# A convolution block on one Trainium2 core: small weights loaded in the first chunks, group matrices loaded by halves and copied, set-up products padded to 64 rows

## The chip, the core and the metric

The kernel runs on one core of a Trainium2 chip. A core has five engines, each with an instruction queue of its own: TensorE (PE in the profile: matrix products from on-chip memory into accumulators; its weight loads are listed as PEld), VectorE (DVE), ScalarE (ACT), GpSimd (POOL) and SyncE (SP), which here only issues DMAs. An engine waits for another, or for a DMA, by semaphores. The DMAs issued by SyncE, ScalarE and GpSimd are carried out by 16 DMA engines. On-chip memory has 128 partitions; an image's channels or pixels lie along them.

The metric is the time of one execution on the device in microseconds (us), and of several runs the median.

## What is computed

Sixteen images of 192 channels and 64x64 pixels in float32 go through two layers. The reference, cut to what matters:

```python
h = layer_norm_over_channels(x)
projected, gate = split(conv1x1(h, in_proj_w, in_proj_b))        # 192 -> 2 x 192
projected = depthwise_3x3(projected, dw_k)
scanned = sum_d mix[d] * scan(projected * iscale[d], decay[d])   # left, right, down, up
local = depthwise_3x3(projected, le_k)
mixed = gelu(batch_norm((scanned + local) * sigmoid(gate)))
x = x + conv1x1(mixed, out_proj_w, out_proj_b)
x = x + fc2(gelu(fc1(layer_norm_over_channels(x))))              # 192 -> 768 -> 192
# second layer
t = relu(norm(mean_over_pixels(x) @ w1.T))
taps = (t @ w2.T + b2) * mask                                    # four taps per channel and image
out = depthwise_3x3(x, taps) + bias
```

The change touches how the weights of `conv1x1(in_proj)` and of the depthwise convolutions are prepared and loaded, not what is computed from them.

## The kernel before

The program has three stages, written one after the other.

**First stage** (lines 278 to 643): normalisation and input projection. The work is cut into 64 chunks, n = 0 to 63; four chunks make a block, and 16 blocks cover all images. The loop at line 617 emits, for each chunk n, in this order on every queue:

- `load_a(n + 3)` (line 502): six DMAs of 128 KB bring the pixels of the chunk three ahead into one of four buffers xa, three issued by SyncE and three by GpSimd. It waits until chunk n - 1 is done with the buffer.
- the stores of the block before. In a block's first chunk these are `store_first` (line 565) and parts 0 and 1 of `store` (line 580), in its second, third and fourth chunk one further part each. Half of the DMAs are issued by SyncE, half by GpSimd. So the last store of a block is issued in the fourth chunk of the next one.
- `turn(n + 1)` (line 515): 24 TensorE transposes of the next chunk, for its variance.
- `project(n, ...)` (line 537): four groups of six matmuls with 64-row operands and 128-column weights into accumulators of which two alternate (`ps_pj0`, `ps_pj1`). VectorE (line 555) and ScalarE (line 556) scale each group and write it into the block's buffer: `stg` for even blocks, part of `mid` for odd ones. Each is one buffer: block 12 writes `stg` again, which block 10 filled and which is free when the stores of block 10 have read it. Block 12 begins at n = 48, block 13 at 52, block 14 at 56.
- the functions that `beside(n, f)` (line 458) put down for this chunk: they come last in it.

These functions prepare the rest of the program. `diagonals`, `gate_bias`, `decay_rows`, `projection_bias` (line 349), `tap_sums`, `columns` (370), `sums_across` (375) and `conv_bias` (381) build biases from small matmuls in chunks 2 to 23. `projection_bias` has nine matmuls of 64x64 weights with one moving column; `conv_bias` runs three times (n = 19, 21, 23) with operands of three rows, `indt` and `svt`, which lie in the room of a later weight, `wf1`. In the trace one float32 matmul is two records, with a weight load of its own each. `vector` and `store_vector` build vectors of convolution taps and decays and store them in device memory (`dv_d`, `lv_d`).

From these vectors `load_dm(g)` (line 216) and `load_lm(g)` (line 223) load the banded matrices of channel group g: every partition reads a run that begins one place earlier than its neighbour's. `dm` (64 rows by 64 columns for 3 x 8 channels) is needed on partitions 0 to 63 and again, the same data, on 64 to 127; half 0 is issued by SyncE, half 1 by GpSimd. For `lm` the two halves hold different channels. `load_weights(k)` (line 111) loads the small weights of later stages, all issued by SyncE: k = 0 output projection, k = 3 and 4 squeeze weights and parameters, k = 1 and 2 the large ones.

**Second stage** (lines 646 to 863): depthwise convolution, scans and gate for 24 groups of eight channels, in 96 steps k of two channels. `depthwise(k)` multiplies by `dm`, `scans(k)` runs on VectorE with `tables(k)` made by ScalarE, `local` and `vertical` multiply by `lm`, `gate` multiplies and stores. Step k = 0 also has `hidden_bias` and `squeeze_rows`. `depthwise(4)`, the first to read group 1's matrices, is emitted in step k = 2.

**Third stage** (from line 866): output projection, second normalisation, hidden layer and the second layer's convolution. The change does not touch it.

The order on every engine is that of the program text; nothing is reordered by a planner.

Of the kernel before, what the change touches and what calls it, by code (L numbers as in the profile page):

```python
# [22 lines left out]
AF = mybir.ActivationFunctionType  # L23
# [4 lines left out]
C = 192  # L28
# [28 lines left out]
def conv_block_kernel(ctx: ExitStack, tc: tile.TileContext, x, prm, w_in, w_out, w_fc1, b_fc1, w_fc2, w1, bn1, w2, out):  # L57
    nc = tc.nc
# [5 lines left out]
    HALF = (slice(0, 64), slice(64, 128))  # L64
# [23 lines left out]
    pt3 = cp.tile([128, 3, NPRM], F32, tag="pt3", name="pt3")  # L88
# [54 lines left out]
    def squeeze_rows(pr):  # L143

        nc.tensor.matmul(pr[:, 0:2 * RED], ones[0:RED], sq_d.rearrange("p k r -> p (k r)"), start=True, stop=True)
        nc.vector.tensor_mul(w1t, w1t, pr[:, 0:RED].unsqueeze(1).broadcast_to([128, 3, RED]))
        nc.vector.tensor_copy(c0, pr[:, RED:2 * RED])
# [57 lines left out]
    mats = [{"dm": ce.tile([128, 3, HW, GC], F32, tag=f"dm{i}", name=f"dm{i}")} for i in range(2)]  # L205
# [10 lines left out]
    def load_dm(g, halves=(0, 1)):  # L216
        for i in halves:
# [2 lines left out]
            src = bass.AP(v.tensor, v.offset, [[GC, HW], [128 * GC, 3], [1, HW * GC]])  # L220
            (nc.sync, nc.gpsimd)[i].dma_start(mats[g % 2]["dm"][q].rearrange("p k m c -> p k (m c)"), src)

    def load_lm(g, halves=(0, 1)):
        n = GC // 2
        for i in halves:
            q = HALF[i]
            v = lv_d[g, i, :, 0:1, :]
            src = bass.AP(v.tensor, v.offset, [[n, HW], [128 * n, 5], [1, HW * n]])
            (nc.sync, nc.gpsimd)[i].dma_start(lm_of(g)[q].rearrange("p k m c -> p k (m c)"), src)
# [48 lines left out]
    with ExitStack() as stage:  # L278
# [3 lines left out]
        lo = slice(0, 64)  # L282

        w0 = place[:, 0:NFC * C].rearrange("p (t n) -> p t n", t=3)
        room = wf1.rearrange("p t m -> p (t m)")
        cut = lambda p, at_, n: room[0:p, at_:at_ + n]
        dg = cut(64, 768, 576).rearrange("p (t k n) -> p t k n", t=3, k=3)
        lnb = cut(64, 1344, 384).rearrange("p (t n) -> p t n", t=3)
        mean_w = cut(64, 0, 128)
        indt, svt = cut(3, 1984, 128), cut(3, 2112, C)  # L290
        dec = ka.tile([64, 3, 4], F32, tag="dec", name="dec")
        bp = ka.tile([64, 3], F32, tag="bp", name="bp")
        sv = ka.tile([64, 3, 3, 3], F32, tag="sv", name="sv")
# [2 lines left out]
        def bank():  # L296
            return psa.tile([128, CH], F32, tag="pj0", name="pb", bufs=2)
# [51 lines left out]
        def projection_bias():  # L349
            pbp = bank()  # L350
            for t in range(3):
                for u in range(3):
                    nc.tensor.matmul(pbp[lo, t:t + 1], w0[lo, u, 64 * t:64 * t + 64], pt3[lo, u, LN1B:LN1B + 1],
                                     start=(u == 0), stop=(u == 2))
            nc.vector.tensor_add(bp, pbp[lo, 0:3], pt3[lo, :, INB])
            nc.vector.memset(ind, 1.0)
            nc.vector.tensor_add(ind[:, 1:2], ident[:, 63:64], ident[:, 127:128])
            nc.vector.tensor_add(ind[:, 2:3], ident[:, 0:1], ident[:, 64:65])

        def tap_sums(t):  # L360
# [6 lines left out]
            nc.gpsimd.tensor_scalar_mul(sv[:, t], sv[:, t], bp[:, t:t + 1])  # L367
            nc.gpsimd.tensor_scalar_mul(sv[:, t, :, 1:3], sv[:, t, :, 1:3], -1.0)

        def columns():  # L370
            pi = bank()
            nc.tensor.transpose(pi[0:3, 0:128], ind, ident)
            nc.scalar.activation(indt, pi[0:3, 0:128], AF.Copy)

        def sums_across(k):
            pr = bank()
            for t in range(3):
                nc.tensor.transpose(pr[0:3, 64 * t:64 * t + 64], sv[:, t, k], ident[lo, lo])
            nc.scalar.activation(svt, pr[0:3, 0:C], AF.Copy)

        def conv_bias(k):
            pq = bank()
# [75 lines left out]
        def beside(n, f, *args):  # L458
            side.setdefault(n, []).append((f, args))
# [6 lines left out]
        beside(7, projection_bias)  # L466
        for t in range(3):
            beside(8 + t, tap_sums, t)
        beside(8, columns)
        for k in range(3):  # L470
            beside(18 + 2 * k, sums_across, k)
            beside(19 + 2 * k, conv_bias, k)
        for k, n in enumerate((13, 14, 15, 16, 24, 32, 33, 34)):
# [3 lines left out]
                    beside(n + j, ready, j // 2, j % 2)  # L477
                    beside(n + 1 + j, runs, j // 2, j % 2)
            beside(n + (5 if k == 4 else 1), store_vector, k)
        for k in (0, 3, 4):  # L480
            beside(40 + k, load_weights, k)
        for h in range(2):
            beside(46 + 4 * h, load_dm, 0, (h,))
            beside(54 + 4 * h, load_lm, 0, (h,))
        beside(60, load_dm, 1)
        beside(61, load_lm, 1)
        beside(62, load_weights, 1)
        beside(50, squeeze_scale)
# [128 lines left out]
        for n in range(n_ac):  # L617
# [11 lines left out]
            h = AR // 2 if n == 0 else 0  # L629
# [16 lines left out]
    with ExitStack() as stage:  # L646
# [11 lines left out]
        def load_pg(g, queue=nc.sync, i0=0, i1=n_half):  # L658
            s = grp[g]
            s["pg"] = pg_even if g % 3 == 0 else pg_odd[g % 3 - 1]  # L660
            if g:
                d = [lo_ <= g < hi_ for lo_, hi_ in PARTS].index(True)
                lo_ = (g - PARTS[d][0]) * GE
                queue.dma_start(s["pg"].rearrange("p n k c j -> p n (k c j)")[:, i0 * NB:i1 * NB],
                                pg_d[d][i0:i1, :, :, lo_:lo_ + GE].rearrange("i b p e -> p (i b) e"))
# [29 lines left out]
        def tables(k):  # L695

            bst[k]["tab"] = []
            for d in range(2):
                tab = wb.tile([128, 2 * CH], F32, tag=f"tab{d}", name=f"tab{d}")
                nc.scalar.activation(tab.rearrange("p (n h) -> p n h", h=HW), mask[:, d].broadcast_to([128, n_img_all, HW]),  # L700
                                     AF.Copy, scale=dec_b[:, d, k:k + 1])
                bst[k]["tab"].append(tab)
# [28 lines left out]
        def vertical(k):  # L731
            for d in range(2):
                lmul(k, 3 + d, lambda h, ih: bst[k]["v"][d][h, ih], lambda a: a, False, d == 1)
# [81 lines left out]
        for k in range(-2, n_bp + 1):  # L815
            if k == -2:
                tables(0)
            elif 0 < k + 1 < n_bp:
                tables(k + 1)
            if k >= 1:  # L820
                vertical(k - 1)
                gate(k - 1)
                g, c = divmod(k, hp_)
                if c == 0 and 0 < g < NCG - 1:
                    load_lm(g + 1)
                if c == 0 and g == 3:
                    load_weights(2)
                if c == 0 and g + 2 < NCG:
                    load_pg(g + 2)
                if c == hp_ - 2 and g + 2 < NCG:  # L830
                    load_dm(g + 2)
            if 0 <= k + 1 < n_bp:
                scans(k + 1)
            if k + 2 < n_bp:
                depthwise(k + 2)
            if 0 <= k < n_bp:
                local(k)
                sigmoid(k)
            if k == 0:
                pb_h = psb.tile([128, 2, CH], F32, tag="d", name="pb_h", bufs=2)  # L840
                hidden_bias(pb_h)
                squeeze_rows(pb_h[:, 0, HCH:CH])
            if k in (1, 3, 5):
                scale_hidden(k // 2)
            if k == n_bp - hp_:

                nc.gpsimd.dma_start(w2t, w2[:, 0:NTAP, :])
                load_y(0, y_low, (nc.sync,), (0, 1))
                load_x2(0)
                load_x2(1)  # L850
            if k == n_bp - hp_ // 2:
                load_y(0, y_low, (nc.sync,), (2,), LASTC)
# [467 lines left out]
    for n in range(n_ch + 1):  # L1320
        p, c = divmod(n, NCH)
# [159 lines left out]
```

## Time and profile before

| | |
|---|---|
| median of three runs | 3539.12 us (3538.75 to 3540.4) |
| the profiled execution | 3536.52 us |
| its span, first to last instruction | 3534.7 us |
| mean granted TensorE clock | 0.997 of full speed |
| first stage | to about 582 us |
| second stage | about 582 to 1250 us |
| third stage | from there to the end |

The page gives busy times and shares of the span for each engine, then the chain of work that ended last: from the last instruction back, at each step, to what released it. A group of instructions is written with its line, engine and operation, and the tiles as out<-in; x48 is the count. A bracket after a line of the timeline is the idle time of that engine before it and the engine or DMA to which the wait is put down; that name is inferred. Matmul lines overlap, since matmuls are pipelined: distances are taken from start to start. Lines SPq are DMA issues of SyncE; the time there is that of the issue, not of the transfer.

### The profile page before, as it was taken

The page shows a single profiled execution, that of the slowest core. Times are in us where ns is not written, and L with a number is a line of the kernel's source. Part 1 is how long each engine was busy: PE and PEld are TensorE (multiplying, and loading weights), DVE is VectorE, ACT ScalarE, POOL GpSimd, SP SyncE. Part 2 cuts the span into 40 slices and gives each one's busy share as a digit, 9 for nine tenths or more (in the row PEclk, how much of TensorE's full clock was granted, in tenths as well). Part 3 has the DMA queues.
Part 4 walks back from the last instruction along what each step waited for, and adds up shares of the span by engine and source line. Part 5 has one row for each costly group of instructions (what it writes and reads, how often), then busy time and mean ns, then how long its engine had stood idle before and what let it go on. Part 6 is the DMA issues. An engine that isn't in the chain of part 4 may idle for free.

```text
span 3534.7 us, 78563 instructions
## 1 busy us (share of the span) xinstructions
PE 3505.9 (99%) x33158; PEld 1910.7 (54%) x33158; DVE 2740.9 (78%) x4669; ACT 1840.2 (52%) x2087; POOL 1171.4 (33%) x1302
## 2 busy tenths in 40 slices
PE   9999999999999999999999999999999999999998
PEld 7666966566666644444444444444444444444444
DVE  7888777999999975557777777777677777767766
ACT  4444446888888854344444535444444444454543
POOL 3545432111111133333333334343333333343433
PEclk9999999999999999999999999999999999999999
DMA  6999999999999941112222222222222222222213
GB/s 178 271 271 279 274 273 303 302 287 280 281 287 281 250 113 37 39 52 61 70 75 68 71 62 82 60 73 65 77 61 70 72 70 67 65 82 58 76 34 90
DMA packets 288745, 492.00 MB, mean 139 GB/s; under 512 B 24752, under 2 KB 182824, under 8 KB 288392
## 3 DMA queue, kind: packets, MB, share of 16 engines
q1 hardware_dynamic: 246548, 341.57, 35.6%
q0 software_dynamic: 40912, 144.37, 14.2%
q8 instruction: 261, 4.28, 0.5%
q10 hardware_dynamic: 932, 1.03, 0.1%
q14 instruction: 92, 0.75, 0.1%
HBM read 284.95 MB, written 197.92 MB: 137 GB/s over the span
## 4 chain that ended last, share of the span: by engine, by line
PE 97%; DVE 1%; DMA 1%; SPq 0%; ACT 0%; issue 0%; ACTq 0%; POOL 0%; DVEq 0%
PE ps_f L1062 28%; PE ps_f L907 19%; PE ps_pj L550 13%; PE ps_l L721 12%; PE ps_s L907 7%; PE ps_d L677 7%; PE ps_o L962 5%; PE ps_o L955 2%; PE ps_xt L521 1%; PE ps_m L991 1%; PE ps_v L991 1%; DMA xa<-in_x_dram 1%; DVE o L66 0%; DMA low<-lv_d 0%; SPq L508 0%
## 5 line engine op out<-in xcount | busy, mean ns | idle before, releaser
L1062 PE MATMUL ps_f<-h,wf 64*64 64x512 f32 (+1 forms) x9240 | 1014.9, 589 | 0.0
L1064 ACT ACTIVATE gl<-ps_f,bf 128x1024 f32<-128x1024 f32 x384 | 428.2, 1115 | 1080.8 <-PE ps_f L1062 1078.5
L1062 PEld LDWEIGHTS ps_f<-h,wf 64*64 64x64 f32 x9240 | 347.1, 133 | 598.1 <-issue 573.8
L907 PE MATMUL ps_f<-gl,place 128*64 128x256 f32 (+1 forms) x3072 | 528.3, 486 | 1.1 <-ACT rs L1043 1.1
L550 PE MATMUL ps_pj<-wi,xa 64*128 64x384 f32 x3072 | 516.2, 487 | 7.4 <-DVE stg L555 7.1
L550 PEld LDWEIGHTS ps_pj<-wi,xa 64*128 64x128 f32 x3072 | 334.7, 188 | 153.4 <-DVE stg L555 9.8
L1097 POOL TENSOR_TENSOR gl<-gl 128x512 f32<-128x512 f32 x192 | 308.9, 1636 | 158.8 <-PE ps_f L907 158.6
L907 PEld LDWEIGHTS ps_f<-gl,place 128*64 128x64 f32 x3072 | 220.4, 137 | 222.4 <-issue 147.4
L1087 POOL COPY turn<-o 128x1 f32<-128x1 f32 x84 | 16.6, 197 | 821.3 <-DVE o L66 821.3
L1093 POOL TENSOR_TENSOR t<-gl 128x512 f32<-128x512 f32 x192 | 246.4, 1283 | 88.8 <-ACT gl L1064 44.4
L1095 POOL TENSOR_TENSOR t<-gl,t 128x512 f32<-128x512 f32 x192 | 247.5, 1289 | 44.1 <-ACT gl L1064 30.9
L66 DVE SCALAR_TENSOR_TENSOR o<-ximg,taps,o 128x1024 f32<-128x1024 f32 x180 | 231.8, 1288 | 4.9
L712 DVE TENSOR_TENSOR_SCAN v<-tab,q 128x1024 f32<-128x1024 f32 x96 | 218.3, 2274 | 5.6 <-ACT q L692 5.6
L714 DVE TENSOR_TENSOR_SCAN v<-tab,q 128x1024 f32<-128x1024 f32 x96 | 217.6, 2267 | 0.0
L508 POOL DMA_DIRECT2D xa<-in_x_dram x192 | 120.7, 635 | 276.7 <-PE ps_pj L550 237.5
L700 ACT ACTIVATE tab<-mask,dec_b 128x1024 f32<-128x1024 f32 x192 | 209.8, 1145 | 0.4 <-DMA pg_d<-stg 0.4
L1120 DVE SCALAR_TENSOR_TENSOR ximg<-ps_f,pt,ximg 128x256 f32<-128x256 f32 (+1 forms) x176 | 96.7, 549 | 145.6 <-PE ps_f L907 145.6
L556 ACT ACTIVATE stg<-ps_pj,rsa 128x384 f32<-128x384 f32 x128 | 119.1, 938 | 162.5 <-PE ps_pj L550 143.8
L556 ACT ACTIVATE mid<-ps_pj,rsa 128x384 f32<-128x384 f32 x128 | 119.3, 934 | 153.7 <-PE ps_pj L550 147.2
L968 DVE SCALAR_TENSOR_TENSOR ximg<-ps_o,pt,low 128x256 f32<-128x256 f32 x264 | 113.0, 480 | 94.4 <-PE ps_o L962 90.1
L962 PE MATMUL ps_o<-low,wo 128*64 128x256 f32 x1536 | 181.7, 385 | 1.8 <-ACT low L935 1.8
L528 DVE BATCH_NORM_STATS2 st<-ps_xt 128x6 f32<-128x192 f32 x512 | 171.8, 336 | 4.5 <-PE ps_xt L521 3.9
(274 smaller groups left out, 5657.7 us busy)
## 6 DMA issues: line engine op xcount, KB each, us to landing
low<-in_x_dram SPq DMA_DIRECT2D x128, 384.0 KB
out_dram<-o SPq DMA_DIRECT2D x172, 256.0 KB
mid<-pg_d SPq DMA_DIRECT2D x8, 4096.0 KB
low<-mixed_d SPq DMA_DIRECT2D x116, 256.0 KB
low<-pg_d SPq DMA_DIRECT2D x7, 4096.0 KB
pg_o<-pg_d SPq DMA_DIRECT2D x7, 4096.0 KB
xa<-in_x_dram POOLq DMA_DIRECT2D x192, 128.0 KB, 5.2
xa<-in_x_dram SPq DMA_DIRECT2D x192, 128.0 KB
```

Source lines behind the costliest of these rows:

```text
L66: nc.vector.scalar_tensor_tensor(o, in0, scalar, in1, ALU.mult, ALU.add, **kw)
L550: nc.tensor.matmul(ps[i], pixels(n, t, g)[q], wi[q, t].rearrange("p g k c -> p (g k c)"), start=(t == 0), stop=(t == 2))
L556: nc.scalar.activation(stag[blk][1][:, :, j], ps[1], AF.Copy, scale=rs[:, g, 1:2])
L677: nc.tensor.matmul(dst(ps[o, ih]), mats[g % 2]["dm"][q, di + 1, :, ch], src(s["pg"][q, :, 0, ch]), start=(di == 0), stop=stop)
L721: nc.tensor.matmul(dst(bst[k]["ps"][o, i]), lm_of(g)[q, m, :, c], src(q, ih), start=start, stop=stop)
L907: nc.tensor.matmul(ps[q], w(i), rhs(i), start=start, stop=stop, **kw)
L962: nc.tensor.matmul(ps[wh][q].rearrange("p (r w) -> p r w", w=32), wo[:, 64 * t:64 * t + 64], cols(rows(s["mx"][:, i]))[:, :, wh], start=fi ...
L1062: nc.tensor.matmul(pf[o, i, x], wf1[q, t, m0:m0 + 64], s["h"][q, t, x], start=(t == 0), stop=(t == 2))
L1064: nc.scalar.activation(gl, pf, AF.Gelu, bias=bf1[:, m:m + 1])
L1093: sub(t1[:, m], b12(m), b11(m))
L1095: sub(t2[:, m], b22(m), t1[:, m])
L1097: sub(b12(m), b22(m), b12(m))
```

## The change

Five things change:

- The small weights (`load_weights` 0, 3 and 4) are loaded beside chunks 0, 1 and 2 instead of 40, 43 and 44.
- The first group's matrices: `load_dm(0)` loads half 0 alone, beside n = 47 instead of 46; half 1 (it was at n = 50) is made by a new ScalarE copy, `copy_dm(0)`, beside n = 52. `load_lm(0)` moves from n = 54 and 58 to 51 and 55.
- For group 1, `load_dm(1)` at n = 60 loads half 0 alone, and `copy_dm(1)` stands in step k = 0 of the second stage. The groups from 2 on are loaded as before.
- `projection_bias` uses 128 columns of weights instead of 64; the upper 64 results are not used.
- `indt` and `svt` get 64 rows. `clear` (beside n = 7) zeroes them; rows 0 to 2 are filled as before, and `conv_bias` multiplies over all 64.

```diff
+    def copy_dm(g):
+
+        dm = mats[g % 2]["dm"].rearrange("p k m c -> p (k m c)")
+        nc.scalar.activation(dm[HALF[1]], dm[HALF[0]], AF.Copy)
...
-        indt, svt = cut(3, 1984, 128), cut(3, 2112, C)
+        indt, svt = cut(64, 1984, 128), cut(64, 2112, C)
...
-                    nc.tensor.matmul(pbp[lo, t:t + 1], w0[lo, u, 64 * t:64 * t + 64], pt3[lo, u, LN1B:LN1B + 1],
+                    nc.tensor.matmul(pbp[:, t:t + 1], w0[lo, u, 64 * t:64 * t + 128], pt3[lo, u, LN1B:LN1B + 1],
...
+        def clear():
+            nc.gpsimd.memset(indt, 0.0)
+            nc.gpsimd.memset(svt, 0.0)
+
         def columns():
...
-            nc.scalar.activation(indt, pi[0:3, 0:128], AF.Copy)
+            nc.scalar.activation(indt[0:3], pi[0:3, 0:128], AF.Copy)
...
-            nc.scalar.activation(svt, pr[0:3, 0:C], AF.Copy)
+            nc.scalar.activation(svt[0:3], pr[0:3, 0:C], AF.Copy)
...
+        beside(7, clear)
         beside(8, columns)
...
-        for k in (0, 3, 4):
-            beside(40 + k, load_weights, k)
+        for n, k in enumerate((0, 3, 4)):
+            beside(n, load_weights, k)
+        beside(47, load_dm, 0, (0,))
+        beside(52, copy_dm, 0)
         for h in range(2):
-            beside(46 + 4 * h, load_dm, 0, (h,))
-            beside(54 + 4 * h, load_lm, 0, (h,))
-        beside(60, load_dm, 1)
+            beside(51 + 4 * h, load_lm, 0, (h,))
+        beside(60, load_dm, 1, (0,))
...
                 squeeze_rows(pb_h[:, 0, HCH:CH])
+                copy_dm(1)
```

## The prediction, made before the changed kernel ran

> **What bounds the kernel now.** First the page: TensorE is busy for 99% of the span and the chain that ended last is TensorE for 97%.
>
> ```profile
> PE 3505.9 (99%) x33158; PEld 1910.7 (54%) x33158; DVE 2740.9 (78%) x4669; ACT 1840.2 (52%) x2087; POOL 1171.4 (33%) x1302
> ...
> PE 97%; DVE 1%; DMA 1%; SPq 0%; ACT 0%; issue 0%; ACTq 0%; POOL 0%; DVEq 0%
> ```
>
> So work taken off another engine is worth nothing; only matmul time, or a gap between matmuls, counts. Second the chain in order of time, around 440 us, for the gaps in the first stage (start, length, what):
>
> ```profile
> 428.11 7.67 PE ps_pj L550 x47
> ...
> 436.64 1.86 PE ps_pj L550 x11
> 438.51 5.43 DMA xa<-in_x_dram
> ...
> 443.94 0.93 DVE stg L555
> ...
> 444.92 6.44 PE ps_pj L550 x24
> ...
> 452.10 7.80 PE ps_pj L550 x48
> 460.63 7.79 PE ps_pj L550 x48
> ```
>
> An undisturbed chunk takes 460.63 - 452.10 = 8.53 us. Counting back from the last chunk's end (580.25), chunk n=48 starts at 436.64 and n=49 at 452.10: 15.46 us, 6.9 too many. TensorE stood idle 4.35 us, and its next 24 records took 6.44 us instead of half of 7.80. n=48 opens block 12, which writes the single buffer stg again; VectorE and ScalarE wait there until block 10's last store, issued in n=47, has read it. The name xa on the wait is the inference; what decides is on SyncE's queue in the timeline:
>
> ```profile
> 412.24 1.79 SPq L126 DMA_DIRECT2D b<-in_bn_dram  x1
> 414.08 2.04 SPq L127 DMA_DIRECT2D pv<-in_prm_dram  x1
> 416.17 4.28 SPq L129 DMA_DIRECT2D pv<-in_prm_dram  x2
> 420.63 2.54 SPq L508 DMA_DIRECT2D xa<-in_x_dram  x3
> ...
> 432.81 1.54 SPq L221 DMA_DIRECT2D dm<-dv_d  x1
> 434.53 2.51 SPq L508 DMA_DIRECT2D xa<-in_x_dram  x3
> 437.08 1.25 SPq L583 DMA_DIRECT2D pg_d<-stg  x2
> ```
>
> SyncE issues the loads of n=45 at 420.63; GpSimd, with the same loads, did so at 410.59. The small loads queued at n=44 cost 8.2 us of SyncE (412.24 to 420.45), the group matrix at n=46 another 1.5, and so the store of n=47 is out at 438.33. The other boundaries show the rule: from the end of SyncE's last issue to the release of stg it is 4.1 us at n=32 (297.84 to 301.97), 4.8 at n=40 (365.55 to 370.38), 5.6 at n=48, 5.0 at n=56 (511.02 to 515.99). n=40 costs TensorE nothing; n=48 is late by what SyncE is late. The same at n=56: chunks 54 to 56 take 522.03 - 494.79 = 27.24 us, 1.6 over three undisturbed; there load_lm of n=54 (503.89, 1.43 us) stands before the last store.
>
> Third the windows, one block of four chunks each; after PEclk come DMA share and GB/s:
>
> ```profile
> 333.50:367.70 34.20, 34.20 (x278) 31.77 (x277) 27.31 (x85) 14.43 (x21) 13.54 (x24) 1.00 1.00 290
> 367.70:401.80 34.10, 34.10 (x294) 33.88 (x292) 27.82 (x85) 15.10 (x21) 14.05 (x25) 1.00 0.95 275
> 401.80:436.60 34.80, 34.80 (x311) 34.58 (x308) 28.59 (x85) 15.83 (x21) 14.32 (x25) 1.00 0.99 268
> 436.60:477.70 41.10, 36.75 (x291) 24.45 (x290) 28.66 (x92) 15.30 (x22) 14.53 (x26) 0.92 0.89 266
> ```
>
> The DMA engines are nearly full as well, yet the block at share 1.00 kept TensorE going. This is the doubt in my forecast.
>
> Fourth the small products, in the timeline of TensorE:
>
> ```profile
> 192.16 0.29 PEld L383 LDWEIGHTS pb<-wf 3*128 3x128 f32 x2 [0.54 <-DVE mva L529]
> 192.17 0.59 PE L383 MATMUL pb<-wf 3*128 3x192 f32 x2
> 192.68 0.96 PE L521 MATMUL ps_xt<-ident,xa 64*128 64x64 f32 x24
> 193.48 7.96 PE L550 MATMUL ps_pj<-wi,xa 64*128 64x384 f32 x48
> ```
>
> The weight load of the 3-row product waits 0.54 us; those of L353 and L372, also of another shape than the projection's 64*128, wait 0.55 and 0.54; those of L327 and L342, of the projection's shape, wait for nothing.
>
> [...] 4.35 us idle, then 2.5 us lost, clock 0.92 in that block; n=56, with a shorter gap, keeps 1.00. [...]
>
> **The change part by part.**
>
> Small loads from n=40, 43, 44 to n=0, 1, 2. Ten DMAs leave SyncE where they took 6.1 (n=40), 2.0 (n=43) and 8.2 us (n=44). They come where no store exists yet: from 25.6 to 59.8 us the DMA share is 0.51. Their 318 KB are 2 us at the 155 GB/s of the start; ten issues of 0.6 us (the shortest at L123) are 6 us of SyncE in three chunks, behind loads that have two chunks of lead, since xa has four buffers. Cost 0; without that cover, two chunks, the 6 us would count. mean64's memset goes along on GpSimd: a 128x192 memset is 0.28 us, 0 here.
>
> load_dm(0): half 0 goes from n=46 to n=47, where it is issued after that chunk's store; half 1 (GpSimd, n=50) goes. With both edits SyncE reaches the store of n=47 as in n=39: 5.7 us after chunk 39's start at 359.8. From 428.11 that is 433.8, plus 4.8 gives 438.6, against 438.3 when VectorE wants stg. VectorE waited 0.61 at n=40 and TensorE lost nothing. Gain 6.9 at n=48; bounds 4 and 6.9. Next late is then TensorE itself.
>
> load_lm(0): halves from 54 and 58 to 51 and 55. SyncE loses the 1.43 us ahead of the store of n=55: 509.0 + 5.0 = 514.0 against 513.6 wanted. But half 1 now follows GpSimd's store of n=55, and its 320 KB are 1.2 us of all DMA engines at 280 GB/s, beside SyncE's store. VectorE's wait of 2.79 cost 1.6, so 1.2 are free; with 1.6 left I keep 0.5 of the stall. Gain 1.1; bounds -1 and 1.6.
>
> copy_dm: an ACTIVATE 64x1536. [...] the trace's 1024 elements with a scale took 1.145. In n=52 it stands before the next chunk's evacuations; from the end of the square root to the next of them ScalarE has 1.7 us (428.42 to 430.13). In the second stage it follows sigmoid(0) at 597.0, so tables(2) end at 600.7 instead of 599.2; the scan takes them at 602.89, and ScalarE idles 3.83 us before 603.01. Cost 0; without cover 1.5 each. For group 1, half the load (384 KB, 1.4 us of DMA) and 0.65 us of GpSimd at 553 go, in a stretch where TensorE waits for nothing: 0.
>
> conv_bias, 3 rows to 64, three times. From the last projection's start to the next: 193.48 - 184.22 = 9.26, over 8.53 by 0.73. Gate bias, of the wide shape, starts six 192-column records in 0.98 us (67.43 to 68.41), so two take 0.33[...]. Gain 0.4 each, 1.2; bounds 0.3[...] and 1.5.
>
> projection_bias, 64 to 128 columns. It adds 89.41 - 79.59 - 8.53 = 1.3 now, at 0.0625 us a record. Wide records with one moving column start every 0.06 us at L165, 64-column ones every 0.105 at L342: 18 are 1.1 to 1.9. Take 1.4: loss 0.1; bounds a gain of 0.2, a loss of 0.6.
>
> clear: two memsets, at most 0.5 us, in GpSimd's 6.87 us of idleness before 87.89: 0. columns and sums_across keep their operands.
>
> Sum: 6.9 + 1.1 + 1.2 - 0.1 = 9.1 us. The second stage starts from TensorE's end and no later wait is shown before its steady pitch, so it passes on. The profiled execution took 3536.52 (span 3534.7 and 1.8 around it), so 3525.6 span and 3527.4; against the median of 3539.12, 3530.0.
>
> **The rivals.** (B) Part of the stall moves. The blocks from 367.7 to 477.7 hold 103.4 us of DMA time (share by length). Less 2.4 for the small loads (268 GB/s at 0.99 against 290 at 1.00 is 7% of 34.8 us, an estimate) and 0.3 for the matrices, 100.7 must fit into three undisturbed blocks, 102.4. Without the stall's pause the queues never drain, so n=52 or n=56 gives 3 to 5 us back: 3534. For it: 0.99 and 1.00; against it: n=40, after the block at 1.00. (C) It does not do what it says: n=48 was late for full rings, not for SyncE's order. Then only the 768 KB saved count (2.7 us at 280 GB/s) and the products' 1.1: 3535.3. Against it: SyncE's 10 us behind GpSimd. (D) Slower: the backlog is carried on [...] at n=52 and at n=56, each with the cold clock, 6.9 each: 13.8 - 6.9 - 1.6 - 1.1 = 4.2 more, 3543.3. It decides once SyncE's last store before each comes out over 4 us later than the 5.7 after its chunk's start. For it: lm half 1 beside that very store; against it: needs it twice.
>
> **How the numbers follow.** Forecast (A) 0.65, own range 3527.5 to 3533; B 0.18, C 0.10, D 0.07. 0.2% is 7.1 us, about what a measurement of this kernel can tell from no change. A passes it in nine of ten cases: 0.58, and B adds 0.01. Slower 0.07, the rest 0.34. The range takes B and C in: 3527 to 3536.
>
> **What would show it.** Right: chunk 48 at 8.5 us and no clock below 1.00 before 580; SyncE's loads within 2 us of GpSimd's at n=44 to 48; L383 without idle before it and chunks 19, 21, 23 at 8.9; first stage's end near 571. Wrong: VectorE waiting for stg or mid over 1.2 us at n=48, 52 or 56; chunks 0 to 3 over 8.6; the scans of the second stage waiting for tables.

## The result: 9.2 us gained, most of it at one chunk

| | before | changed |
|---|---|---|
| median of ten executions each, same chip | 3539.19 us | 3530.47 us |
| lowest to highest | 3529.32 to 3542.7 | 3524.74 to 3536.67 |
| ratio, with its 95% interval | | 0.9974 (0.9964 to 0.9984) |
| the profiled execution | 3536.52 | 3533.97 |
| its span | 3534.7 | 3532.2 |

The ratio is a gain of 9.2 us, with an interval from 5.7 to 12.7; it is not the quotient of the two medians, which lie 8.7 us apart. The forecast was 3530.0. The two profiled executions differ by only 2.5 us, because the changed kernel's is one of its slower ones and that of the kernel before lies 2.7 us below its median. So the traces have to show two things: what the edits did, and what the rest of the program gave or took in that one execution.

The first and fourth part of the changed kernel's page, busy time by engine and the chain's shares, look as before:

```profile
PE 3508.4 (99%) x33158; PEld 1925.6 (55%) x33158; DVE 2741.3 (78%) x4669; ACT 1843.2 (52%) x2089; POOL 1168.5 (33%) x1302
...
PE 98%; DVE 1%; DMA 1%; ACT 0%; issue 0%; SPq 0%; ACTq 0%; POOL 0%
```

TensorE still bounds the kernel, and its busy time even grew by 2.5 us. The chain of waits around 440 us shows where the gain lies (start, length, what; line 561 is the old 550):

```profile
429.54 7.68 PE ps_pj L561 x47
...
438.08 7.68 PE ps_pj L561 x47
...
446.61 7.68 PE ps_pj L561 x47
...
455.15 7.68 PE ps_pj L561 x47
```

From start to start these are 8.54, 8.53 and 8.54 us; the second is chunk n = 48, which took 15.46 before. The DMA wait and the slow records after it are gone. In the timeline, SyncE's queue from n = 47 on (start, length of the issue, source line):

```profile
429.02 3.44 SPq L519 DMA_DIRECT2D xa<-in_x_dram  x3
432.51 1.55 SPq L594 DMA_DIRECT2D pg_d<-stg  x2
434.10 0.98 SPq L221 DMA_DIRECT2D dm<-dv_d  x1
437.37 3.02 SPq L519 DMA_DIRECT2D xa<-in_x_dram  x3
```

The store of n = 47 is out at 434.06, about 4 us before chunk 48 starts on TensorE; before it was out 1.7 us after that point. The group matrix now stands behind it. GpSimd issues the same chunks' loads at 429.10 and 437.63, so SyncE is no longer late. The windows of the three blocks from n = 47 on (clock granted, DMA share and GB/s are the last three columns):

```profile
429.50:463.70 34.20, 34.20 (x291) 33.97 (x290) 27.99 (x85) 15.28 (x21) 13.91 (x25) 1.00 0.97 280
463.70:497.80 34.10, 34.10 (x290) 33.82 (x289) 28.65 (x92) 16.85 (x23) 13.82 (x25) 1.00 1.01 289
497.80:532.70 34.90, 33.75 (x273) 25.54 (x272) 27.05 (x85) 14.49 (x20) 14.15 (x25) 1.00 0.98 281
```

The clock stays at 1.00, and the stretch that held the stall now has a DMA share of 0.97. The DMA engines are as full as in the blocks ahead of it; the store that frees `stg` now comes in time. In the third window TensorE is idle for 34.90 - 33.75 = 1.15 us; the loss there is at n = 56.

A sum over the whole first stage comes from ScalarE's square roots, one for each chunk. Here are their distances, wherever the two kernels differ (us):

```
place                               before  changed  difference
first chunk                          6.62     8.02    +1.40
before the first square root                          +0.56
projection_bias                      9.88    10.57    +0.69
conv_bias, three times               9.25     9.01    -0.24 each
the chunk before each of them        8.97     9.01    +0.05 each
n = 32 and n = 36, block starts     18.65    17.99    -0.66 together
n = 48                              15.49     8.54    -6.95
n = 56                              10.15    10.01    -0.14
end of the first stage             580.25   574.59    -5.66
```

The profiled execution then gave back another 3.2 us that no edit asks for: by the second stage's steady steps it led by 4.38, at the start of the third stage by 2.96, at the end by 2.5. The first 1.2 us went in the second stage's first steps, where the granted clock fell. The windows of the changed kernel:

```profile
588.00:594.00 6.00, 5.24 (x50) 3.22 (x52) 3.12 (x5) 5.94 (x6) 0.00 (x0) 0.65 1.06 381
594.00:600.00 6.00, 6.00 (x64) 2.82 (x60) 4.71 (x5) 2.45 (x5) 0.64 (x1) 0.78 1.01 421
```

`copy_dm(1)` stands in that stretch, but another execution of the same kernel (experiment 4) has 1.00 in both windows and is 7.1 us ahead of the kernel before after them; the kernel before has 0.72 from 594 to 600 itself. The next 1.4 us went at the end of the second stage, with 0.72 from 1248 to 1254: the two matmuls of line 817 took 2.06 us there, and 1.10 in the kernel before. Experiments 4, 8, 9 and 11 look at further losses of one execution.

### The profile page after: what moved, and what is told of

It is laid out like the page before. It is cut to its first block, busy times and chain, and to the rows that moved or that the text cites. A ratio compares the mean times of both kernels' runs of the same rounds, so it can differ in the third digit from the quotient of the medians.

```text
span 3532.2 us, 78570 instructions
## 1 busy us (share of the span) xinstructions
PE 3508.4 (99%) x33158; PEld 1925.6 (55%) x33158; DVE 2741.3 (78%) x4669; ACT 1843.2 (52%) x2089; POOL 1168.5 (33%) x1302
## 4 chain that ended last, share of the span: by engine, by line
PE 98%; DVE 1%; DMA 1%; ACT 0%; issue 0%; SPq 0%; ACTq 0%; POOL 0%
PE ps_f L1074 28%; PE ps_f L919 19%; PE ps_pj L561 14%; PE ps_l L732 12%; PE ps_s L919 7%; PE ps_d L688 7%; PE ps_o L974 5%; PE ps_o L967 2%; PE ps_xt L532 1%; PE ps_m L1003 1%; PE ps_v L1003 1%; DMA xa<-in_x_dram 0%; DVE o L66 0%; DVE v L723 0%; DVE v L725 0%
## 5 line engine op out<-in xcount | busy, mean ns | idle before, releaser
L561 PEld LDWEIGHTS ps_pj<-wi,xa 64*128 64x128 f32 x3072 | 360.3, 188 | 123.4 <-DVE stg L566 2.8
```

What stands on the lines that cost most here:

```text
L561: nc.tensor.matmul(ps[i], pixels(n, t, g)[q], wi[q, t].rearrange("p g k c -> p (g k c)"), start=(t == 0), stop=(t == 2))
```

## The experiments

Theory A is the forecast's: SyncE's order made n = 48 late, and undoing that order is the gain. Its rivals were B (part of the stall moves to a later block), C (the DMA engines full, not the order) and D (a backlog that stalls two blocks). After the result, the slow start and the scatter between executions were open as well. Each ratio is to the kernel before, taken on the same chip.

**1. The small loads alone**, on the kernel before:

```diff
-        for k in (0, 3, 4):
-            beside(40 + k, load_weights, k)
+        for n, k in enumerate((0, 3, 4)):
+            beside(n, load_weights, k)
```

> The kernel before with the small weights (load_weights 0, 3, 4) moved to chunks 0, 1, 2 and nothing else. Theory 1 (the stall at n=48 is SyncE's lateness): the 8.2 us ahead of n=45 are gone, the group matrix at n=46 still costs 1.5, so VectorE waits about 2.1 us at n=48 and TensorE loses 0.9 instead of 6.9: 6 us faster than before. Rival 1 (full DMA engines, the bytes of the group matrix): stall of 4 us or more stays at n=48. Rival 2 (the loads in the first chunks slow the start, as the changed kernel's trace seems to show): chunk 0 ends 2 us later than in the trace of before, 8.0 instead of 6.6 us between the first two square roots; then only 4 us faster. If that is the chance of the TensorE clock, it may show here or not, and must show in a kernel with the old placing as well.

Measured: 3530.22 us against 3538.6, ratio 0.9983 (0.9975 to 0.999). The chain of waits of this kernel:

```profile
428.28 7.79 PE ps_pj L550 x48
...
436.81 7.83 PE ps_pj L550 x48
...
445.38 7.80 PE ps_pj L550 x48
```

Chunk 48 takes 8.57 us from start to start. The stall is gone although `load_dm` still stands at n = 46, ahead of the store; the 0.9 us still expected from it did not come. The last store was out 2.4 us before the chunk's start, and VectorE waited 1.21 us for `stg`. Moving ten small loads is therefore enough for the whole gain at n = 48 in this trace. No later block got slower either (n = 56 took 9.02), which speaks against B, and against C.

**2. The matrices alone**, on the kernel before: `load_dm(0)` half 0 at n = 47 with the copy at 52, `load_lm(0)` at 51 and 55, half of `load_dm(1)` with its copy.

```diff
-            beside(46 + 4 * h, load_dm, 0, (h,))
-            beside(54 + 4 * h, load_lm, 0, (h,))
-        beside(60, load_dm, 1)
+        beside(47, load_dm, 0, (0,))
+        beside(52, copy_dm, 0)
+            beside(51 + 4 * h, load_lm, 0, (h,))
+        beside(60, load_dm, 1, (0,))
...
+                copy_dm(1)
```

> The kernel before with the group matrices loaded and copied as in the changed kernel, weights at chunks 40 to 44 and products as before. Theory 1: the 1.5 us of n=46 go, the lateness from n=44 stays; SyncE's store of n=47 comes about 3 us late instead of 4.5, VectorE waits 3.6, TensorE loses 2.4 at n=48 without the cold clock: 4.5 us faster. Rival 1: the stall at n=48 is gone (0 to 0.5). Both: n=56 as in the changed kernel, 1.4 to 1.6.

Measured: 3534.28 us, ratio 0.9995 (0.9984 to 1.0005), so no change that can be told. Chunk 48 took 12.26 us: about half of the stall is left. SyncE's queue in this kernel, in the timeline:

```profile
416.30 2.15 SPq L126 DMA_DIRECT2D b<-in_bn_dram  x1
...
437.25 2.12 SPq L589 DMA_DIRECT2D pg_d<-stg  x2
439.41 0.86 SPq L221 DMA_DIRECT2D dm<-dv_d  x1
```

and VectorE's write to `stg` at n = 48, also in the timeline, in the kernel before and then in this one:

```profile
443.94 0.92 DVE L555 TENSOR_SCALAR stg<-ps_pj,rsa 128x384 f32<-128x384 f32 x1 [5.85 <-DMA xa<-in_x_dram]
443.39 0.94 DVE L561 TENSOR_SCALAR stg<-ps_pj,rsa 128x384 f32<-128x384 f32 x1 [4.88 <-DMA pg_d<-mid]
```

The store is out at 439.37, 2.3 us after the chunk's start, with the matrix behind it: still as late as in the kernel before (1.7), yet VectorE waits 4.88 here and 5.85 there. So the time from SyncE's issue to the release of `stg` is not a constant. Over the six traces in which VectorE waited for that release at n = 48 it ran from 3.7 to 6.3 us. TensorE at n = 48, in the timeline:

```profile
444.38 4.14 PE L556 MATMUL ps_pj<-wi,xa 64*128 64x384 f32 x24 [3.40 <-DVE stg L561]
```

It waited 3.40 us in place of 4.35, and the 24 records after the wait took 4.14 in place of 6.44, for which the windows of the kernel before have a granted clock of 0.64 (444.92 to 451.40). So the stall is shorter here by a quicker release and by faster records behind it, not by an earlier store: the new place of the matrix is not what halved it. n = 56 took 8.52 in this execution.

**3. The padded products alone**, on the kernel before: the diff's edits to `indt`, `svt`, `clear`, `columns`, `sums_across` and `projection_bias`.

> The kernel before with the padded products and clear alone. From the trace of the changed kernel: chunk 7 longer by 0.7 us, the three conv_bias chunks shorter by 0.25 each with 0.05 lost in the chunk before each: sum 0.1 slower, no difference in the time; the stall at n=48 stays at 6.9. [...]

Measured: 3537.8 us, ratio 0.9999 (0.9991 to 1.0007). In the trace `projection_bias` cost 0.7 us more and the three `conv_bias` together 0.6 less, so the padding is worth nothing in sum. n = 48 took 15.80. The timeline of TensorE in the changed kernel shows why the gain is small:

```profile
194.40 0.19 PEld L392 LDWEIGHTS pb<-wf 64*128 64x128 f32 x1
194.72 0.32 PE L392 MATMUL pb<-wf 64*128 64x192 f32 x1
194.72 0.19 PEld L392 LDWEIGHTS pb<-wf 64*128 64x128 f32 x1
194.88 0.32 PE L392 MATMUL pb<-wf 64*128 64x192 f32 x1
195.90 8.01 PE L561 MATMUL ps_pj<-wi,xa 64*128 64x384 f32 x48
```

The projection ahead of this product, in the timeline of the kernel before and then of the changed one:

```profile
184.22 8.01 PE L550 MATMUL ps_pj<-wi,xa 64*128 64x384 f32 x48
186.87 8.01 PE L561 MATMUL ps_pj<-wi,xa 64*128 64x384 f32 x48
```

The 0.54 us wait ahead of the weight load is gone, as expected. But it was hardly TensorE's time: in the kernel before it ended at 192.16, while the matmuls of the projection ahead ran to 192.23. From the start of that projection to the first record of the product it was 192.17 - 184.22 = 7.95 us and is now 194.72 - 186.87 = 7.85, only 0.10 less. Behind it, from the first record to the next projection, it is 195.90 - 194.72 = 1.18 us, against 1.31 before (193.48 - 192.17). The two make up the gain of a product. What else holds it up there was not tried. And for `projection_bias`:

```profile
89.34 1.84 PE L358 MATMUL pb<-pt,place 64*128 64x1 f32 x16
```

Eighteen such records now start 0.107 us apart, in place of 0.063, which costs 0.8 us. The end of the wait ahead of them, 0.55 us at the weight load, gave back only 0.1, again from projection start to first record (8.01 and 7.91 us).

**4. The changed kernel once more**, unaltered, for a second trace:

> The changed kernel once more, unaltered, for a second trace. Theory 1 with chance at the start: the first two square roots 6.6 us apart or 8.0, n=48 undisturbed, n=56 1.4 lost, chunk 7 and conv_bias as in the first trace to 0.05 us. Rival 2: 8.0 again.

Measured: 3529.3 us over 19 executions, ratio 0.9976 (0.9968 to 0.9983). The profiled execution took 3535.24, and its chunks agree with those of the first trace (8.54 at n = 48, 10.58 at `projection_bias`); n = 56 took 9.10 in place of 10.01. What differs is one step of the second stage. In the chain of waits:

```profile
608.06 25.16 DMA dm<-dv_d
...
633.36 4.83 PE ps_d L688 x39
```

This is the first read of group 2's matrices, which every kernel here loads whole in the second stage. TensorE's records wait for them; the timeline puts the idle time at 5.72 us, and the next 39 records take 4.83 in place of 2.6, on a clock of 0.57 by the windows from 633.0 to 638.2. The step lasts 14.83 us in place of 6.89. SyncE's part in the timeline:

```profile
607.62 0.39 SPq L675 DMA_DIRECT2D mid<-pg_d  x1
608.06 9.27 SPq L221 DMA_DIRECT2D dm<-dv_d  x1
```

and GpSimd's:

```profile
615.54 1.73 POOL L780 DMA_DIRECT2D mixed_d<-low  x1 [18.78 <-DVE low L766]
```

The load of `dm` is put behind 4 MB for `mid`, and takes 9.27 us to issue alone; while it does, GpSimd starts the 2 MB store of group 0. Across the profiled kernels, sorted by how long after SyncE's load of `mid` that store was issued (us):

```
run                        4 MB load to store    lost in this step
e7                               7.1                   8.2
e4                               7.9                   7.9
e6                               8.3                   5.3
e1                               8.6                   1.1
e5                               8.7                   1.1
e3                               9.1                   0.4
before                           9.2                   0
e2                               9.3                   0
e8                               9.6                   0
changed, first trace            10.3                   0
e10                             11.3                   0
```

Two of these rows are the same kernel, and the two that lose most have little in common with each other that others lack. So this is a matter of phase in one execution, and it can explain 8 of the 12 us by which executions of one kernel differ. Of the eight traces with early small loads five lost 1.1 us or more, of the three with all of them at their old places none lost over 0.4. Three are too few to tell whether the change makes this loss likelier; it is not excluded.

**5. The changed kernel without the padding of `projection_bias`:**

```diff
-nc.tensor.matmul(pbp[:, t:t + 1], w0[lo, u, 64 * t:64 * t + 128], pt3[lo, u, LN1B:LN1B + 1],
+nc.tensor.matmul(pbp[lo, t:t + 1], w0[lo, u, 64 * t:64 * t + 64], pt3[lo, u, LN1B:LN1B + 1],
```

> The changed kernel with projection_bias back at 64 columns of weights. If that padding costs what the traces of the changed kernel show, the chunk after chunk 7 is 0.7 us shorter (10.57 to 9.88 between square roots) and the whole up to 0.7 us faster than the changed kernel, too little for the times to tell. Start: 6.6 to 8.0 us between the first two square roots, by chance (theory 1); 8.0, or at least over 6.8, by the early loads (rival 2).

Measured: 3528.01 us (6 executions), ratio 0.9969 (0.9958 to 0.9981). The chunk takes 9.88 again, so this edit alone loses 0.7. The first two square roots, 7.18 us apart, fit both accounts of the start. The medians' 2.5 us below the changed kernel is within the scatter.

**6. The changed kernel with both halves of the matrices loaded**, with no copies:

```diff
-        beside(47, load_dm, 0, (0,))
-        beside(52, copy_dm, 0)
+        beside(47, load_dm, 0)
...
-        beside(60, load_dm, 1, (0,))
+        beside(60, load_dm, 1)
...
-                copy_dm(1)
```

> The changed kernel with both halves of the group matrices loaded (n=47 and n=60, SyncE and GpSimd) and no copies by ScalarE. Theory: the copies hide nothing and cost nothing; 768 KB of loads come back, 2.7 us of DMA beside work that has room for it; the same time within 1 us, n=48 undisturbed, n=52 under 0.3 us. If the bytes are what counts (rival 1), n=48 or n=52 loses 2 us or more.

Measured: 3529.94 us (7), ratio 0.9979 (0.9968 to 0.9991). Chunk 48 took 9.50, where no loss was expected, VectorE having waited 2.12 us for `stg`. The saved half can thus be worth up to 1 us there, by one trace. The medians don't tell the two kernels apart. The copy itself, in ScalarE's timeline of the changed kernel:

```profile
480.78 0.29 ACT L544 ACTIVATE rsa<-mva,eps 128x8 f32<-128x8 f32 x1
481.09 1.48 ACT L226 ACTIVATE dm<-dm 64x1536 f32<-64x1536 f32 x1
482.79 0.94 ACT L567 ACTIVATE mid<-ps_pj,rsa 128x384 f32<-128x384 f32 x1 [0.22 <-PE ps_pj L561]
```

It fits between the square root and the next evacuation, which still waits for TensorE.

**7. One of the three small loads back at n = 44:**

```diff
-        for n, k in enumerate((0, 3, 4)):
+        for n, k in ((0, 0), (1, 3), (44, 4)):
```

> The changed kernel with load_weights(4) alone back at n=44: 51 KB in rows of 16 and 200 bytes, 0.2 us at 280 GB/s, but four issues that took 8.2 us of SyncE there. Theory 1 (SyncE's queue): a stall comes back at n=48, 2 to 4 us, less than 6.9 since neither the other loads nor the group matrix stand beside it. Rival 1 (bytes on the DMA engines): no stall at n=48, under 0.5 us.

Measured: 3533.13 us, ratio 0.9985 (0.9977 to 0.9992), and chunk 48 took 8.60: no stall. This missed what was expected of SyncE's queue, and is what the expectation named for the bytes. SyncE's queue in the timeline:

```profile
409.84 2.35 SPq L126 DMA_DIRECT2D b<-in_bn_dram  x1
412.24 1.98 SPq L127 DMA_DIRECT2D pv<-in_prm_dram  x1
414.26 4.38 SPq L129 DMA_DIRECT2D pv<-in_prm_dram  x2
418.81 2.85 SPq L519 DMA_DIRECT2D xa<-in_x_dram  x3
...
434.85 1.28 SPq L594 DMA_DIRECT2D pg_d<-stg  x2
```

and VectorE at n = 48:

```profile
439.84 0.92 DVE L566 TENSOR_SCALAR stg<-ps_pj,rsa 128x384 f32<-128x384 f32 x1 [1.26 <-DMA pg_d<-stg]
```

The four loads hold SyncE for 8.8 us (8.2 in the kernel before), and the loads of n = 45 come out at 418.81, 7.7 us after GpSimd's. In the three traces with a stall that distance is larger, 9.7 to 10.5 us. But three chunks later the store is out at 436.13, 1.0 us before the chunk's start: SyncE had worked most of its lateness off. With the loads of n = 40 and 43 as well (experiment 2) it did not. The profiled execution, at 3535.64, lost 8.2 us in the second stage's step of experiment 4. The median lies 2.7 us above the changed kernel's, and whether all sixteen executions kept n = 48 free, one trace can't show.

**8. A warm start.** Experiment 5's kernel with 20 more matmuls, whose results nothing uses, ahead of the first chunk's transposes:

```diff
+        for _ in range(20):
+            nc.tensor.matmul(idle[:, 0:128], ones, ones, start=True, stop=True)
```

> As e5, with 20 more matmuls of ones (128x128, results unused) ahead of the first transposes, where TensorE waits for the first pixels. If the slow first chunk is the cold clock after this gap, its first 24 records take 4.09 us and not up to 6.63, and the first two square roots are 6.6 us apart at most; up to 2 us faster than e5 in those executions that begin cold. If the early loads slow the start through the DMA engines, 8.0 stays.

Measured: 3528.2 us, ratio 0.9974 (0.9965 to 0.9983). The first 24 records of chunk 0 took 4.09 us, in place of 6.63 in the changed kernel. But the 20 matmuls, 40 records, took 4.73 us and held up the transposes until 15.97, so by the second square root it stood 2.8 us behind the kernel before. Too many. The changed kernel's start, in TensorE's timeline:

```profile
14.14 0.69 PE L532 MATMUL ps_xt<-ident,xa 64*128 64x64 f32 x8 [2.46 <-DMA xa<-in_x_dram]
14.63 6.63 PE L561 MATMUL ps_pj<-wi,xa 64*128 64x384 f32 x24
```

and in the windows of the changed kernel:

```profile
14.00:19.00 5.00, 4.86 (x22) 2.97 (x24) 3.56 (x16) 0.26 (x1) 0.00 (x0) 0.50 1.18 221
```

The granted clock is 0.50 there. In the kernel before, with a wait of 1.79 us (and one of 0.20 earlier), the same window has 1.00 and the same records took 4.09.

**9. Group 0's store on SyncE**, in the changed kernel, behind the load of group 2's matrices instead of beside it:

```diff
-                parts = ((nc.gpsimd, 0, n_half),) if g < NCG - 1 else
+                parts = ((nc.gpsimd if g else nc.sync, 0, n_half),) if g < NCG - 1 else
```

> The changed kernel with the 2 MB store of group 0's result (line 780) issued by SyncE, behind its loads of group 2, instead of GpSimd. Five of the traces with the early small loads lost 1.1 to 8.2 us at step 8 of the second stage waiting for group 2's loads, the others 0 to 0.4; the loss goes with the time between SyncE's issue of group 2's 4 MB and GpSimd's issue of this store: 9.1 us and over none, 8.6 to 8.7 1.1, 8.2 5.3, 7.9 and 7.1 about 8. Theory 3 (the store takes the DMA engines from the load): no wait at step 8, 6.9 us between the scans there, the same time as the changed kernel's best executions, 1 to 4 us under its median. Rival: the load is late for its own reasons (the 16 stores ahead of it on SyncE); then waits of 1 to 8 us come as before.

Measured: 3527.24 us (6), ratio 0.9968 (0.9956 to 0.9979). The step took 6.89 us in this trace: nothing lost.

**10. The small loads one chunk later**, at n = 1, 2 and 3:

```diff
-            beside(n, load_weights, k)
+            beside(n + 1, load_weights, k)
```

> The changed kernel with the small loads at chunks 1, 2, 3, so that SyncE issues none of them before the first chunk has run (the load ahead of them waits for it). Rival 2 (early loads slow the start): the first 24 projection records take 4.1 to 5.4 us, as in the three traces with late loads (4.09, 4.09, 5.37), and not 5.5 to 6.6 as in the six with early ones. Theory 1 (chance of the TensorE clock): anything from 4.1 to 6.6. The rest of the first stage as in the changed kernel; n=48 undisturbed.

Measured: 3530.73 us, ratio 0.9975 (0.9969 to 0.9982), and in TensorE's timeline:

```profile
14.44 0.69 PE L532 MATMUL ps_xt<-ident,xa 64*128 64x64 f32 x8 [2.59 <-DMA xa<-in_x_dram]
14.92 6.65 PE L561 MATMUL ps_pj<-wi,xa 64*128 64x384 f32 x24
```

The start is as slow as with the loads in chunk 0, and the granted clock from 14 to 19 us is 0.50 here too. So the early loads are not what slows it.

**11. Experiment 5's kernel with experiment 9's edit and eight extra matmuls**, again without a use for their results:

> The changed kernel without the padding of projection_bias, with group 0's store on SyncE, and with 8 matmuls of ones before the first transposes (20 were 4.73 us and 1.8 too many, so 1.9 us now, which ends before the first pixels are there). If theory 3 and the cold start both hold: first 24 records 4.09 us, chunk 7 without the 0.7, step 8 without a wait: 0.7 + 1 to 2.5 + 1 to 4 us under the changed kernel, about 3525. If neither holds, as the changed kernel, 3529 to 3530.

Measured: 3527.82 us, ratio 0.9965 (0.9955 to 0.9975). TensorE's timeline:

```profile
10.97 2.05 PE L624 MATMUL pb<-ones 128*128 128x128 f32 x16
...
14.52 0.46 PE L532 MATMUL ps_xt<-ident,xa 64*128 64x64 f32 x8 [0.85 <-DMA xa<-in_x_dram]
14.81 4.09 PE L561 MATMUL ps_pj<-wi,xa 64*128 64x384 f32 x24
```

Eight matmuls fit into the wait for the pixels, the granted clock from 14 to 19 us is 1.00, and the first 24 records take 4.09. The step of the second stage took 6.89. The profiled execution took 3524.84, but the median stays above the 3525 expected, and one execution took 3539.72.

**12. Experiment 5's kernel with experiment 9's edit**, no extra matmuls:

> The changed kernel without the padding of projection_bias and with group 0's store on SyncE, no extra matmuls. Theory 3: a third trace without a wait at step 8 (6.9 us), whatever the clock does ahead of it; the time of e11, about 3527.5, and its slow executions no slower than 3533. Rival (the load is late for its own reasons): in half of all traces a wait of over 1 us at step 8, and executions up to 3538 as in the changed kernel.

Measured: 3528.02 us, ratio 0.9973 (0.9964 to 0.9982). The chain of waits in the second stage:

```profile
607.29 19.26 DMA dm<-dv_d
...
626.68 2.90 PE ps_d L688 x40
```

TensorE still waited 0.76 us for the matrices, and the step took 7.92, where 6.9 was expected. With the store out of the way the load landed 19.26 us after its issue, against 25.16 in experiment 4. By these two traces the store costs this load some 6 us when it comes early, and the load has no spare time even without it.

Did any version beat the changed kernel? Six versions without the moved store (the changed one and experiments 4, 5, 6, 8, 10) have 74 executions with a median of 3529.8; the three with it have 30, at 3527.6. Their ratios' intervals overlap and the chips differ, so 2 us better is possible and not shown.

## Why the prediction was right, and where it was not

**The total and the main step hold.** The forecast was 3530.0 with 6.9 us from n = 48; the median is 3530.47 and the trace gives 6.95 there. Of its signs, chunk 48 at 8.5 us, SyncE abreast of GpSimd from n = 44, and no wait for `stg` over 1.2 us at n = 48 (0.61, put down to TensorE) all came. "No clock below 1.00 before 580" holds around the stall but not at the start, where it was 0.50. Two signs of being wrong came as well. VectorE, in the timeline at n = 48 and n = 56:

```profile
440.14 0.89 DVE L566 TENSOR_SCALAR stg<-ps_pj,rsa 128x384 f32<-128x384 f32 x1 [0.61 <-PE ps_pj L561]
510.45 0.94 DVE L566 TENSOR_SCALAR stg<-ps_pj,rsa 128x384 f32<-128x384 f32 x1 [2.63 <-DMA xa<-in_x_dram]
```

The wait of 2.63 us at n = 56 (2.79 before) shows that this part of the forecast failed. Chunks 1 and 2 took 9.39 and 8.62, over the limit of 8.6, but the kernel before has 9.37 and 8.65: that sign could not tell the two apart.

**Within that step, the sentence "n=48 is late by what SyncE is late" fell.** It put 8.2 us of the lateness on the small loads of n = 44 and 1.5 on the matrix of n = 46, added up. Experiment 7 has the first alone and experiment 1 the second alone: by one trace each, neither costs TensorE 0.1 us. The lateness only becomes a stall when the loads of n = 40 and 43 come on top (3.7 us lost with the matrix moved, 6.9 to 7.3 with it in place). The later part of that rule, 4.1 to 5.6 us from issue to release, ran from 3.7 to 6.3. What the queue needs to catch up three chunks later was not settled beyond these points.

**B, C and D fell.** No later block took over the stall: n = 52 stood at 8.5, and n = 56 no worse than before. C had the DMA engines full of bytes, but the changed kernel's DMA share is 0.97 to 1.01 in those blocks with TensorE undisturbed, and experiment 1, which saves none of the 768 KB of C, removes the whole stall. In every trace with a stall SyncE's store was out after the chunk's start (1.7, 1.7 and 2.3 us), in every trace without one it was out 1.0 us or more before it, n = 48 of experiment 6, with its 1 us, included. D's backlog never formed.

A rival inside A is that the small loads make the DMA engines slower for everyone, and not SyncE's queue alone. GpSimd's transfers go through the same engines: from 409 to 440 us in the kernel before, 44.0% of the time of the 16 DMA engines went to one queue (3.91 MB) and 52.2% to the other (4.23 MB). In that stretch, in the DMA issues of the kernel before and then of the changed one (size of each, median us from issue to landing):

```profile
pg_d<-stg POOLq DMA_DIRECT2D x2, 320.0 KB, 5.2
pg_d<-stg POOLq DMA_DIRECT2D x2, 320.0 KB, 7.0
```

In experiments 2 and 3, with the stall, they took 5.0 and 4.8 us; in experiments 1 and 7, without it, 6.7 and 6.6. GpSimd's loads of 128 KB took 4.5 to 5.2 us in the three traces with the stall and 5.3 to 6.0 in these three without. So what GpSimd issued landed no later where the stall was, and the lateness is that of SyncE's queue. Bytes still count for something: experiment 6 lost its 1 us with SyncE's store out 1.9 us before the chunk. Why short loads hold the queue so long was not tried.

**Term by term of the sum:**

- Small loads at the start, 0: held. The first chunk is slow in the profile, by 1.96 us at its end. Of these, 0.56 come before the first square root, and 0.53 and 0.82 came there in experiments 2 and 3, with the old places. For the rest, experiments 8, 10 and 11 point to the clock, not to the loads: with the loads later the granted clock from 14 to 19 us stayed at 0.50 (experiment 10, 6.65 us for the first 24 records), with extra matmuls ahead it was 1.00 in experiment 11, and the records took 4.09 there and in experiment 8. The prediction counted a loss of clock only behind gaps like the 4.35 us at n = 48, and had not seen that the wait for the first pixels could come with one; how long a wait must be for that is not shown. Its length alone does not tell: the records took 6.63 us behind a wait of 2.46, 6.65 behind 2.59 (experiment 10) and 5.53 behind 2.78 (experiment 12).
- lm at n = 56, 1.1: not shown. The new placing gave 8.52 to 10.01 us over eleven traces, mean 9.15; the old one 10.15, 9.02 and 9.34, mean 9.50. A third of a microsecond at best, inside the scatter. It was read from a single execution.
- `conv_bias`, 1.2: mis-sized. It gave 3 x 0.24 less 3 x 0.05, 0.6. Its wait of 0.54 us was read at the weight load and taken for TensorE's; of that, TensorE got 0.10. What makes that weight load wait is not shown.
- `projection_bias`, -0.1: mis-sized. It lost 0.7, a little beyond the far bound of 0.6. Of two start spacings that the profile offered, 0.06 for wide records with one moving column (line 165) and 0.105 for those with 64 (line 342), a value between was taken. The records took 0.107, though they have one moving column; why they are slower than those of line 165 is not shown.
- Copies and `clear`, 0: held. The copy took 1.48 us, where 1.5 was counted; an ACTIVATE of 1536 elements already takes that in the kernel before (line 1011, 128x1536, 1.484 us). In the second stage `tables(2)` ended at 595.1, and ScalarE then still waited 3.52 us for TensorE.

So the terms that the edits really move are 6.95 + 0.6 - 0.7 + at most 0.3, about 7 us, and not 9.1. The ratio's 9.2 lies 2 us above that, well inside its interval of 5.7 to 12.7. That 9.1 met 9.2 is luck in the last 2 us.

**The end of the first stage near 571 did not come**; it was 574.59. Of the 3.4 us between, 1.96 are the start, 1.0 the misjudged `lm`, 0.6 each `conv_bias` and `projection_bias`, less 0.66 that two other block starts gave. Nor did the lead "pass on" whole: no wait was counted at the second stage's start, but the granted clock from 587 to 604 us was 0.80 in the changed kernel's first trace, 1.00 in its second and 0.90 in the kernel before.

## What to carry to other kernels

A small load can hold its issuer's queue far longer than its bytes suggest (here 51 KB for 5.0 to 8.8 us, in the kernel before at a DMA share of 0.99 from 409 to 419 us), and what matters is who stands behind it: put such loads where the queue has slack, or behind the store that frees a single buffer. A queue that is late once can catch up, as in the one trace of experiment 7 (7.7 us behind GpSimd at n = 45, its store of n = 47 out 1.0 us before the chunk); look for several late items in a row, and don't multiply one item's lateness into a stall. A wait at a weight load need not be a gap between matmuls (0.54 us at the one, 0.10 between the others here): take the distance from matmul to matmul before pricing it. Where one execution shows a loss below a microsecond at a place with full DMA engines, compare it with a second trace before it goes into a sum.

## What was not expected of the hardware

- Four small loads of 51 KB, issued together, held SyncE for 5.0 to 8.8 us (experiments 2, 3, the kernel before, experiment 7); one load of group matrices behind 4 MB held it for 7.8 to 9.3 us over fourteen traces, and in experiment 12 the next load, with the 2 MB store ahead of it, took 13.39 us to issue.
- The first 24 records took anything from 4.09 to 6.65 us, in kernels with the same TensorE instructions up to there, and not in the order of the wait ahead of them: 4.09 behind 1.79 us in the kernel before, 6.63 behind 2.46 in the changed kernel, 6.65 behind 2.59 in experiment 10, 5.53 behind 2.78 in experiment 12.
- A load without spare time that met a 2 MB store made one execution lose 7.9 us in a step where another of the same kernel lost none (experiment 4 and the first trace): 5.72 us of waiting, and 2.2 us in the next 39 records, at a granted clock of 0.57.
